# Two-layer graph attention on one core: the layout in DRAM of the split q and k, and the loads that read it

## The chip, the cores and the metric

One chip is a Trainium2 (trn2); the kernel runs on one of its cores. The metric is device time in microseconds (us) from the start to the end of the program, lower is better. A profile of one execution goes with it. In the profile PE is TensorE, PEld its weight load, DVE is VectorE, ACT is ScalarE, POOL is GpSimd and SP is SyncE; "L543" is line 543 of the kernel, and "SPq" or "ACTq" is an instruction of that engine's queue that issues a DMA.

## What is computed

16 graphs (batches) of 1024 nodes with 256 features each, all in float32, and an integer adjacency matrix for each. Layer 0 has 8 heads of 32 columns:

```python
q, k, v = heads(x @ Wq), heads(x @ Wk), heads(x @ Wv)       # (16, 8, 1024, 32)
e = einsum('whqd,whkd->whqk', q, k)
e = where(e >= 0, e, 0.2 * e)
attn = softmax(where(adj > 0, e, NEG), axis=-1)
h = layernorm(attn @ v, heads side by side)
x = x + layernorm(concat([h, x]) @ Wffn.T)
```

Layer 1 makes two graph attentions, in which the score of a pair of nodes is a sum of one number for each node, then a layer norm with the residual, a feed-forward of 1024 hidden units with ReLU, and a last layer norm with the residual.

## The kernel before

The kernel goes through the 16 batches in order. While the scores of batch b are worked on, the features, the mask and the projections of batch b + 1 are made ready, and what remains of batch b - 1 (output projection, the two graph attentions, feed-forward) is done in between. The order of all instructions on all engines is fixed when the kernel is built: each piece of work is a Python generator that says which engine it wants next and at what cost, and a planner (`Order`, with due times from `AIM`) picks the next one. Buffers are counted by pools of the same planner: a thread takes one and gives it back. At run time every engine, and every queue of an engine that issues DMAs, goes through its own list in order.

**Projections (`qk_part`, L446).** For each batch, each group g of 4 heads, o = 0 for q and 1 for k, and each half of the nodes, PE makes a tile of 128 rows (4 heads of 32 columns) by 512 nodes. ACT writes it rounded to `high` (L463), DVE writes the difference to `low` (L465). Both are buffers of the pool "pair" (18 buffers, 2 KB of each of the 128 partitions), which also holds the adjacency loads `adj_i` (L394, issued by ACT), the feature loads `xr` (L435, issued by ACT) and many intermediates. SyncE stores `high` and `low` to the DRAM tile `qk_halves` (L469), 256 KB each, and the thread gives the two buffers back.

**Stacks (`load_stacks`, L521).** For each head, SyncE makes four loads of 256 KB (L543) from `qk_halves` into the two tiles `qs` and `ks`, of 128 partitions by 1024 nodes each. `qs` holds q's 32 high rows and 32 low rows, twice; `ks` holds k's high rows twice in the upper 64 partitions and k's low rows twice in the lower 64. One matmul over 128 partitions thus gives (high + low of q) times (high + low of k). There are two pairs of stacks, so the loads of head h + 2 can start when the scores of head h are done. The planner prices the four issues at 500 ns each (L533, `load(4)`).

**Scores (`all_scores` L556, `weights` L583).** For each head and each of 8 tiles of 128 keys, two matmuls of 512 columns write 128 x 1024 scores (L576). ACT or DVE scales them by 0.2 (L594, L592; DVE only in batch 0), DVE takes the maximum with the scores (L596), ACT takes the exponential (L599), and GpSimd multiplies by the mask (L603), which needs that half of the mask from all 8 adjacency tiles. PE then multiplies by v (L623), and `after_head` transposes the sums (L649) and divides.

**Beginning.** Batch 0 has nothing before it that could cover its projections, its mask and its first stacks. In it `prepare` (L1008) also loads and folds the other weights ("setup", loads at L283 and L1026 to L1029 on SyncE, PE at L1044 to L1082).

The `general_path` at the end of the file is run only if a check of value ranges fails, and takes no part here.

Of the kernel before, what the change touches and what calls it, by code (L numbers as in the profile page):

```python
# [9 lines left out]
FT = mybir.dt.float32  # L10
# [10 lines left out]
P = 128  # L21
# [156 lines left out]
def on(shared=False, delay=0.0, **costs):  # L178
    return "on", (costs, shared, delay)
# [6 lines left out]
def wait(event):  # L186
    return "wait", event


def fire(event):  # L190
    return "fire", event


def take(pool):
    return "take", pool


def give(pool):
    return "give", pool


def start(thread, aim):
    return "start", (thread, aim)
# [21 lines left out]
def unshifted_path(  # L225
# [8 lines left out]
    nc = tc.nc  # L234
    B, N, D = x.shape
# [3 lines left out]
    DH = D // H  # L239
# [4 lines left out]
    G = 4  # L244
# [19 lines left out]
    dram = ctx.enter_context(tc.tile_pool(name="dram", bufs=3, space=bass.MemoryType.DRAM))  # L264
# [4 lines left out]
    def misc(dtype=FT):  # L269
        return psum.tile([P, HALF], dtype, tag="misc", name="ps_m", bufs=bufs["misc"])  # L270

    def buf(shape, tag, name, dtype=FT):
        return sb.tile(shape, dtype, tag=tag, name=name, bufs=bufs[tag])
# [44 lines left out]
    def load(n=1, latency=3500):  # L318

        return on(SP=500 * n, delay=latency)  # L320
# [59 lines left out]
    scratch = {}  # L380
# [65 lines left out]
    def qk_part(b, g, o, nh):  # L446

        w = (wq, wk)[o]
        cols = slice(nh * HALF, (nh + 1) * HALF)
        for u in range(nh * 2, nh * 2 + 2):  # L450
            yield wait(("xT", b, u))
        yield take("stage")
        yield take("pair")
        yield take("pair")
        yield take("misc")
        pa = misc()
        high, low = (buf([P, HALF], "pair", n) for n in ("high", "low"))
        yield on(PE=1720)
        for dc in range(DC):
            nc.tensor.matmul(pa, w[:, dc, g * P:(g + 1) * P], xTs[b][:, dc, cols],  # L460
                             start=(dc == 0), stop=(dc == DC - 1))
        yield on(ACT=590)
        nc.scalar.copy(high.bitcast(FR), pa)  # L463
        yield on(DVE=690)
        nc.vector.tensor_tensor(low, pa, high, op=OP.subtract)  # L465
        yield give("misc")
        yield load(2)
        for i, part in enumerate((high, low)):
            nc.sync.dma_start(scratch[b, g][o, i, :, cols], part)  # L469
        yield give("pair")  # L470
        yield give("pair")
        yield give("stage")
        yield fire(("qk", b, g, o, nh))

    def project_qk(b, g, t0):
        scratch[b, g] = dram.tile([2, 2, P, N], FT, name="qk_halves")
        for o in range(2):
            for nh in range(NH):
                yield start(qk_part(b, g, o, nh), t0 + (2 * o + nh) * AIM["qk_step"] * SLOT)
# [31 lines left out]
    def project(b, t0):  # L511
        yield take("xT")
        xTs[b] = buf([P, DC, N], "xT", "xT")
        for u in range(NP):
            yield start(x_pair(b, u), t0 + (AIM["x"] + AIM["x_step"] * u) * SLOT)
        yield start(make_mask(b, t0), t0 + 0.5 * SLOT)
        for g in range(H // G):
            yield start(project_qk(b, g, t0 + AIM[("qk0", "qk1")[g]] * SLOT), t0)
            yield start(project_v(b, g, t0 + AIM[("v0", "v1")[g]] * SLOT), t0 + (0.8, 1.0)[g] * SLOT)

    def load_stacks():  # L521


        for b in range(B):
            for h in range(H):
                yield take("stacks")
                both = [sb.tile([P, N], FR, tag=name, name=name, bufs=bufs["stacks"]) for name in ("qs", "ks")]
                stacks[b, h] = both
                for o in range(2):
                    for nh in range(NH):  # L530
                        yield wait(("qk", b, h // G, o, nh))
                d = scratch[b, h // G]
                yield load(4)  # L533
                for o in range(2):
                    for i in range(2):

                        rows = slice((h % G) * DH, (h % G + 1) * DH)
                        if o == 0:
                            src = d[0, :, rows, :]
                        else:  # L540
                            s = d[1, i, rows, :]
                            src = bass.AP(tensor=s.tensor, offset=s.offset, ap=[[0, 2], [N, DH], [1, N]])
                        nc.sync.dma_start(both[o][i * 2 * DH:(i + 1) * 2 * DH, :].bitcast(FT), src)  # L543
                yield fire(("stack", b, h))

# [543 lines left out]
    with tc.manual_schedule():  # L1089
        for dst, w in ((wq, Wq), (wk, Wk), (wv, Wv)):  # L1090
            load_w(dst, w)
        work.add(project(0, -SLOT), 0.0)
        work.add(load_stacks(), 0.0)
        work.add(all_scores(), 0.0)
        work.add(all_values(), 0.0)
        work.add(prepare(), 0.5 * SLOT)
        work.run()
# [308 lines left out]
```

## Time and profile before

| | before |
|---|---|
| time, median of 3 runs | 4614.92 us (4610.21 to 4616.06) |
| span of the profiled execution | 4611.1 us |
| PE busy | 4364.5 us, 95% |
| DVE, ACT, POOL busy | 3267.0, 2895.1, 2451.1 us |
| granted TensorE clock, mean | 0.982 |
| DMA | 343.54 MB, mean 75 GB/s |
| loads of stacks (L543) | 512 of 256 KB, issued by SyncE |
| stores of halves (L469) | 256 of 256 KB, issued by SyncE |

Busy time is a sum over the span; a mean over 4.6 ms does not tell whether all stretches look alike, so views of single stretches go with it. A wait in the profile is put down to the instruction whose end came last before the waiting instruction began. A granted clock below 1.00 means that the matmuls of that stretch ran slower.

### The profile page before, as it was taken

Reading aid. Unit: us, or ns where it says so; the run is one execution under the profiler, and the core shown is the slowest. Engines: PE = TensorE matmul, PEld = TensorE weight load, DVE = VectorE, ACT = ScalarE, POOL = GpSimd, SP = SyncE. Lnnn points to the kernel's source line nnn. Section 1 sums busy time; section 2 is a strip of 40 time slices with the busy share of each in tenths; the row PEclk is TensorE's granted clock in tenths of the full one; section 3 lists DMA queues with packets and bytes.
Section 4 is the critical chain, followed back from the end, with each engine's and each line's share of the span. In section 5 each row is a group of like instructions: output and inputs, shape, how many; then the busy total and the mean of one; then the engine's idle time right before and its main releaser. Section 6 shows DMA issues by size and latency. Waiting matters only on the chain.

```text
span 4611.1 us, 57125 instructions
## 1 busy us (share of the span) xinstructions
PE 4364.5 (95%) x20298; PEld 2930.7 (64%) x20298; DVE 3267.0 (71%) x5246; ACT 2895.1 (63%) x4030; POOL 2451.1 (53%) x1544
## 2 busy tenths in 40 slices
PE   5788899999999999999999999999999999999999
PEld 2344466766667666666766667676666766666587
DVE  2666777777678776777777677777767876777754
ACT  2556567666666666666666666666666666666631
POOL 1565556556555655555456555555655465565710
PEclk7889999999999999999999999999999999999999
DMA  4311212212121221212122121221213122121100
GB/s 136 113 52 64 95 59 82 79 57 99 63 102 57 79 84 61 102 61 95 60 78 84 68 102 61 87 73 66 93 64 106 59 77 83 60 98 44 40 21 20
DMA packets 151940, 343.54 MB, mean 75 GB/s; under 512 B 17504, under 2 KB 20064, under 8 KB 151648
## 3 DMA queue, kind: packets, MB, share of 16 engines
q1 hardware_dynamic: 105568, 255.90, 15.1%
q10 hardware_dynamic: 46080, 83.91, 5.9%
q8 instruction: 164, 2.69, 0.2%
q14 instruction: 128, 1.05, 0.1%
HBM read 239.09 MB, written 100.66 MB: 74 GB/s over the span
## 4 chain that ended last, share of the span: by engine, by line
PE 62%; DVE 17%; DMA 8%; issue 5%; POOL 5%; ACT 3%; SPq 0%; ACTq 0%; POOLq 0%; DVEq 0%
PE ps_a L623 13%; PE ps_s L576 8%; PE ps_m L847 8%; PE ps_m L912 7%; PE ps_m L940 7%; PE ps_m L872 5%; DVE att L810 4%; POOL p L603 4%; DVE att L813 4%; DVE p L596 4%; DMA ks<-qk_halves 3%; DMA adj_i<-in_adj_dram 3%; PE ps_m L757 3%; PE ps_m L725 2%; PE ps_m L728 2%
## 5 line engine op out<-in xcount | busy, mean ns | idle before, releaser
L603 POOL TENSOR_TENSOR p<-p,mask 128x1024 f32<-128x1024 f32 x1024 | 2209.6, 2174 | 1715.5 <-ACT p L599 1547.4
L596 DVE TENSOR_TENSOR p<-p,ps_s 128x1024 f32<-128x1024 f32 x1024 | 1210.2, 1213 | 417.8 <-ACT p L594 417.0
L599 ACT ACTIVATE p<-p 128x1024 f32<-128x1024 f32 x1024 | 1080.8, 1058 | 447.2 <-DVE p L596 412.3
L594 ACT ACTIVATE p<-ps_s 128x1024 f32<-128x1024 f32 x993 | 973.4, 1025 | 223.0 <-PE ps_s L576 179.3
L623 PE MATMUL ps_a<-p,v 128*64 128x512 f32 x4096 | 1020.2, 615 | 50.2 <-POOL p L603 48.2
L576 PE MATMUL ps_s<-qs,ks 128*128 128x512 f32 x2048 | 633.1, 429 | 62.1 <-DVE p L596 37.0
L623 PEld LDWEIGHTS ps_a<-p,v 128*64 128x64 f32 x4096 | 246.0, 137 | 540.7 <-issue 384.7
L576 PEld LDWEIGHTS ps_s<-qs,ks 128*128 128x128 f32 x2048 | 352.3, 191 | 357.9 <-DVE p L596 103.7
L872 PE MATMUL ps_m<-y,att 128*128 128x256 f32 x2048 | 483.3, 382 | 16.3 <-ACT v L497 13.6
L940 PE MATMUL ps_m<-wf,hid 128*128 128x256 f32 x2048 | 475.7, 382 | 9.0 <-ACT xT L309 8.7
L912 PE MATMUL ps_m<-rT,wf 128*128 128x256 f32 x2048 | 475.6, 381 | 0.4 <-DVE rT L368 0.4
L847 PE MATMUL ps_m<-y,att 128*128 128x258 f32 x2048 | 472.4, 381 | 1.5 <-DVE hn L656 1.5
L940 PEld LDWEIGHTS ps_m<-wf,hid 128*128 128x128 f32 x2048 | 380.7, 191 | 77.9 <-issue 15.3
L872 PEld LDWEIGHTS ps_m<-y,att 128*128 128x128 f32 x2048 | 377.4, 190 | 81.9 <-ACT v L497 16.3
L847 PEld LDWEIGHTS ps_m<-y,att 128*128 128x128 f32 x2048 | 386.0, 190 | 65.3 <-issue 4.6
L810 DVE SCALAR_TENSOR_TENSOR att<-first,second 128x1024 f32<-128x1024 f32 x256 | 353.1, 1379 | 82.0 <-ACT first L797 82.0
L912 PEld LDWEIGHTS ps_m<-rT,wf 128*128 128x128 f32 x2048 | 379.4, 191 | 49.5 <-PE ps_m L649 0.8
L813 DVE SCALAR_TENSOR_TENSOR att<-mask,att 128x1024 f32<-128x1024 fp8e4 x256 | 328.0, 1281 | 8.7
L818 ACT ACTIVATE y<-y,check 128x258 f32<-128x258 f32 x256 | 130.8, 511 | 290.1 <-DVE check L816 268.5
L400 DVE TENSOR_SCALAR adj_b<-adj_i 128x512 fp8e4<-128x512 int32 x256 | 226.9, 918 | 99.0 <-DMA adj_i<-in_adj_dram 99.0
L334 POOL TENSOR_SCALAR rs<-mv 128x2 f32<-128x2 f32 (+1 forms) x224 | 57.2, 255 | 416.0 <-DVE mv L331 415.9
L921 ACT ACTIVATE hid<-ps_m,bf 128x256 f32<-128x256 f32 x383 | 163.5, 472 | 132.6 <-PE ps_m L912 104.6
(100 smaller groups left out, 4256.9 us busy)
## 6 DMA issues: line engine op xcount, KB each, us to landing
adj_i<-in_adj_dram ACTq DMA_DIRECT2D x256, 256.0 KB
qs<-qk_halves SPq DMA_DIRECT2D x256, 256.0 KB
ks<-qk_halves SPq DMA_DIRECT2D x256, 256.0 KB
qk_halves<-high SPq DMA_DIRECT2D x128, 256.0 KB
qk_halves<-low SPq DMA_DIRECT2D x128, 256.0 KB
xr<-in_x_dram ACTq DMA_DIRECT2D x64, 256.0 KB
x_kept<-x SPq DMA_DIRECT2D x64, 256.0 KB
x<-x_kept SPq DMA_DIRECT2D x64, 256.0 KB
```

Source lines behind the costliest of these rows:

```text
L576: nc.tensor.matmul(ps[i][:, cols], kk[:, t * P:(t + 1) * P], q[:, cols], start=True, stop=True)
L594: nc.scalar.activation(p, ps, AF.Copy, scale=ALPHA)
L596: nc.vector.tensor_tensor(p, p, ps, op=OP.max)
L599: nc.scalar.activation(p, p, AF.Exp)
L603: nc.gpsimd.tensor_tensor(p, p, mask_of(b, t), op=OP.mult)
L623: nc.tensor.matmul(acc[nh * 64:(nh + 1) * 64, :], v[:, t, c:c + 64], p[:, nh * HALF:(nh + 1) * HALF], start=(t == 0), stop=(t == NT - 1))
L810: nc.vector.scalar_tensor_tensor(e, first[:, 0, :], second[:, j:j + 1], first[:, 1, :], op0=OP.mult, op1=OP.max)
L813: nc.vector.scalar_tensor_tensor(e, mask_of(b, j), -1.0, e, op0=OP.mult, op1=OP.mult, accum_out=sums[:, j:j + 1])
L847: nc.tensor.matmul(pa[:, cols:cols + width], big[:, j, i * P:(i + 1) * P], rows[:, j, :width], start=(j == 0), stop=(j == NT - 1))
L872: nc.tensor.matmul(pa[:, i * D:(i + 1) * D], big[:, j, t * P:(t + 1) * P], y2[:, j, :D], start=(j == 0), stop=False)
L912: nc.tensor.matmul(pa[:, i * 2 * P:(i + 1) * 2 * P], wf1[:, dc, hc * P:(hc + 1) * P], rT[:, dc, :], start=(dc == 0), stop=(dc == DC - 1))
L940: nc.tensor.matmul(pa[:, i * D:(i + 1) * D], hid[hc // 2][:, hc % 2, i * P:(i + 1) * P], wf2[:, hc, :], start=(hc == 0), stop=False)
```

## The change

The dimensions of the DRAM tile `qk_halves` are put in another order: before, [q or k][high or low][128 rows][1024 nodes], and after, [q or k][128 rows][high or low][1024 nodes]. The stores follow it. A load for `qs` reads 64 rows of one piece of DRAM, in which high and low alternate; before it read two blocks of 32 rows. A load for `ks` reads 32 rows, each of them twice in succession; before it read a block of 32 rows, twice. The purpose is that the access patterns of these loads have 64 or 32 rows as outermost dimension and no longer 2. In the stacks the rows stand in another order, the same one in `qs` and in `ks`.

```diff
-            nc.sync.dma_start(scratch[b, g][o, i, :, cols], part)
+            nc.sync.dma_start(scratch[b, g][o, :, i, cols], part)
...
-        scratch[b, g] = dram.tile([2, 2, P, N], FT, name="qk_halves")
+        scratch[b, g] = dram.tile([2, P, 2, N], FT, name="qk_halves")
...
-                        rows = slice((h % G) * DH, (h % G + 1) * DH)
+                        rows = d[o, (h % G) * DH:(h % G + 1) * DH]
                         if o == 0:
-                            src = d[0, :, rows, :]
+                            src = rows.rearrange("d i n -> (d i) n")
                         else:
-                            s = d[1, i, rows, :]
-                            src = bass.AP(tensor=s.tensor, offset=s.offset, ap=[[0, 2], [N, DH], [1, N]])
+                            src = bass.AP(tensor=rows.tensor, offset=rows[:, i, :].offset,
+                                          ap=[[2 * N, DH], [0, 2], [1, N]])
                         nc.sync.dma_start(both[o][i * 2 * DH:(i + 1) * 2 * DH, :].bitcast(FT), src)
```

## The prediction

> **What bounds the kernel now.** I read the page first (TensorE busy 95% of the span, DMA far from full), then busy time by stage, because an average over 4.6 ms hides a start that differs from the rest. Columns of a row: stretch, length, then busy time and instruction count of PE, PEld, DVE, ACT and POOL, granted clock, DMA share, GB/s.
>
> ```profile
> 36.00:64.50 28.50, 4.46 (x15) 1.80 (x15) 2.05 (x4) 2.19 (x5) 0.00 (x0) 0.61 0.41 135
> 64.50:120.00 55.50, 30.96 (x90) 12.18 (x91) 23.38 (x25) 19.11 (x25) 19.11 (x9) 0.72 0.31 101
> ...
> 174.00:205.00 31.00, 17.21 (x71) 6.44 (x70) 16.74 (x20) 16.04 (x20) 19.20 (x10) 0.89 0.36 117
> ...
> 727.00:1000.00 273.00, 267.87 (x1265) 181.24 (x1264) 202.06 (x325) 182.30 (x254) 152.31 (x96) 1.00 0.22 78
> ```
>
> There are two regimes. From about 690 us on, every batch takes 273 us and PE is busy for 267.9 of it at clock 1.00: PE-bound. The list of PE's waits between 1000 and 4003 us (eleven batches) has no DMA in it; it opens with
>
> ```profile
> PE ps_m L409 <- DVE low L465: 17.5, 11, 1.6
> PE ps_m L872 <- ACT v L497: 10.7, 11, 1.0
> ```
>
> that is, one wait of each kind per batch. Before 600 us PE often idles, at a lower clock. So the question is what the loads cost in the first 600 us. Their rate can be read where they run almost alone, in the DMA view of 294 to 334 us (40 slices of 1 us; the loads of one head are issued from 294.92 to 299.4):
>
> ```profile
> DMA  1001111111111111111111110000000000005000
> GB/s 45 0 8 41 37 37 45 49 49 53 53 49 57 49 49 57 49 49 57 49 49 57 49 45 8 0 16 0 0 0 8 0 0 0 0 0 233 29 0 0
> ```
>
> The four loads (4 x 256 KB = 1.05 MB) take until 318 us at 49 to 57 GB/s and a busy share of one tenth: two engines of sixteen. The single 256 KB transfer at 330 us runs at 233 GB/s. The timeline of SyncE shows the second effect: issues stall while the two engines are full, and what comes next in SyncE's order stalls too (a pair of issues costs 1.0 us when nothing blocks).
>
> ```profile
> 37.49 5.79 SPq L543 DMA_DIRECT2D ks<-qk_halves  x2
> ...
> 162.93 6.32 SPq L543 DMA_DIRECT2D ks<-qk_halves  x2
> 169.30 6.72 SPq L283 DMA_DIRECT2D setup<-in_L_gnn_Wffn_dram  x1
> ```
>
> Third, the timelines of PE and ACT show who waits (in brackets: idle time before, and releaser).
>
> ```profile
> 64.49 2.05 PE L576 MATMUL ps_s<-qs,ks 128*128 128x512 f32 x4 [18.25 <-DMA ks<-qk_halves]
> ...
> 192.74 0.69 PE L1044 MATMUL ps_m<-ident,setup 128*128 128x128 f32 x2 [8.63 <-DMA setup<-in_L_gnn_Wffn_dram]
> ...
> 223.68 2.05 PE L576 MATMUL ps_s<-qs,ks 128*128 128x512 f32 x4 [5.82 <-DMA ks<-qk_halves]
> ...
> 579.18 1.12 PE L649 MATMUL ps_m<-ident,ho 128*128 128x128 f32 x4 [8.65 <-ACT v L497]
> ```
>
> ```profile
> 81.52 1.06 ACT L599 ACTIVATE p<-p 128x1024 f32<-128x1024 f32 x1 [6.64 <-DMA qs<-qk_halves]
> ...
> 116.66 1.02 ACT L594 ACTIVATE p<-ps_s 128x1024 f32<-128x1024 f32 x1 [13.38 <-issue]
> ...
> 578.74 0.39 ACT L497 ACTIVATE v<-ps_m 128x256 f32<-128x256 f32 x1 [4.73 <-DMA ks<-qk_halves]
> ```
>
> ACT does not read the stacks. It waits because it issues the adj_i loads (L394) in its own order: such a load needs a "pair" buffer, buffers of that pool also hold "high" and "low" until their store has landed, and the stores share rings with the stack loads. The chain of waits says it for the 13.4 us:
>
> ```profile
> 92.12 23.53 DMA ks<-qk_halves
> 115.64 0.02 issue
> 115.67 0.02 ACTq L394
> ```
>
> **What the Trainium skill says.** "DMA: Bandwidth & Descriptors", section "Why a DMA increments its semaphore by 16 and not by 1": the number of engines is the largest k up to 16 that divides the slowest dimension (size 1 left out) of both access patterns; its "Rules for kernel authors" name a leading broadcast of c copies as confining a transfer to c engines. That gives 2 for both old patterns (outermost 2 against 64 partitions) and agrees with the tenth of busy share above. It gives 16 for the new ones (64 against 64, and 32 against 64); no trace of before shows that. Section "Queues, rings and completion order" of the same page: on each engine descriptors are consumed in ring order, so a store issued behind stack loads waits for its share on those two engines; the two chain lines agree.
>
> **The change, part by part.**
>
> *Loads, 512 of 256 KB.* Bytes, count and issuing engine stay; the engines go from 2 to 16. Cost of a head's four loads now: 24 us. After: from above, 16 times an engine's 53/2 = 26.5 GB/s, 424 GB/s, gives 2.5 us; from below, the stretch 2 to 8 us moves 284 GB/s at share 0.95 with 2 KB rows, 299 GB/s in full, 3.5 us. With issues (4 x 0.5 us) and landing I take 6 us, 5 to 8.
>
> *Stores, 256.* Rows of 2 KB as before, 128 partitions outermost, so their engines stay; only the row pitch in DRAM grows from 4 to 8 KB. I price this at nothing: they land beside compute, which waits on them only through freed buffers. At worst the rate halves, some 1 us more for each.
>
> *Order of rows in the stacks.* q's high and low now alternate with d, and so does k's repeat; the same sum over 128 rows, the same matmuls. The order of instructions does not move, since the planner's price for the loads (L533) is not edited. No wait is added.
>
> *(a) First score, 64.49 us.* Its loads are issued from 36.1 us. After, issues end at 38.1. Ahead are four stores (1.05 MB, issued from 33.2) and two adj_i loads (0.5 MB): with the stacks 2.6 MB, at 300 GB/s about 9 us from 34 us, so landed about 44. Gain 20.
>
> *(b) Head 0, 64.5 to 119 us.* The ACT stall of 6.6 goes (the stores are out by 43, landed before ACT wants buffers). The last mask chunk of batch 0 (adj_i issued at 95.03, used by DVE at 101.99) lands in 5 us in place of 7: 2. The 13.4 us ACT stall hides mostly under four GpSimd products (103.4 to 111.7); the scores at 118.99 would otherwise have gone at 116: 3. Together 11.
>
> *(c) 120 to 307 us.* PE's wait for the setup load, 8.6, goes: that load was issued at 169.3 behind a blocked SyncE and landed behind a head's loads. The ks wait, 5.8, goes. Two mask transposes waiting for adj_b (1.3 and 2.0): 3.2 together. Sum 18. The rest stays: near its end this stretch is spaced by GpSimd (L603, 2174 ns each, POOL busy 139.9 us from 64.5 to 306.6).
>
> *(d) Batch 1, 307 to 690 us.* The 8.65 at 579 goes, as ACT there is held up by the ks loads (6.04 and 4.73 just before). Waits for xr (4.3 at 366, 3.5 at 644) shrink by 3 in all, since the first runs beside a head's loads. Sum 12.
>
> *(e) Clock.* The four matmuls after the 18 us gap take 2.05 us, later ones 1.20. Fewer gaps mean fewer slow restarts: 4 us, an estimate from some five such places.
>
> *(f) Steady batches and tail.* DVE waits for adj_i 99 us in all, which must shrink, but DVE has 71 us free of each 273, and no PE wait there ends in a DMA. Zero.
>
> Sum: 20 + 11 + 18 + 12 + 4 = 65, so 4614.9 - 65 = **4550 us**.
>
> **The rivals.** *Small gain, 4582.* Only waits that PE itself has on these transfers return (18.3 + 5.8 + 8.6 = 33); what ACT and SyncE lost is taken over by GpSimd. For it: several (b) and (c) gaps already end in POOL waits. Against: the last chain lines and the 8.65 at 579 put the hold-up of ACT on these loads.
>
> *Large gain, 4520.* With loads prompt, batch 0 is paced by its engines alone. DVE and POOL each have 140 us of work in 64.5 to 306.6; at 78% of the busier one that is 180 us, not 242: 62, with (a) and (d) 94. For it: the heads' period of 26 to 31 us lies close to the 24 us of a load. Against: from 235 to 307 heads still take 24 us, and PE waits for no load there.
>
> *Slower, 4625 or more.* Stores at the larger pitch, or short full-width bursts in the way of adj_i, hold up the steady batches: it would take 5 us in each of 15 to eat the gain and add 10. For it: a batch has 5.2 us of PE idle time, so no slack on PE. Against: DMA share there is 0.22, and transfers at full width leave the rings sooner. The skill's row on HBM pitch ("Latency and other measured facts") starts its losses from 512 KiB; here it is 8 KB, and no run here shows the loss.
>
> *No change* would need the loads to stay at two engines, for instance if contiguous rows were merged again.
>
> **How the numbers follow.** Forecast 0.60, large gain 0.20, small gain 0.15, no change 0.02, slower 0.03. Faster 0.95, same 0.02, slower 0.03. Range 4500 to 4588: down to a large gain with one more 20 us of the 140 us that PE idles from 36 to 580, up past the small one.
>
> **What would show it.** Right: a head's loads at over 250 GB/s for 3 to 4 us in place of two dozen slices of about 50; issues of ks at 0.5 us each; first score near 44 us; PE's waits for ks and for setup gone; end of batch 0 (306.6 now) near 255; 273 us in each steady batch. Wrong: loads still at 53 GB/s; first score after 55; a steady batch other than 273; or the gaps of (b) and (c) kept, with POOL or DVE as releaser.

## The result, and the profile after

| | before | after |
|---|---|---|
| time, median of 6 runs each | 4611.02 us | 4532.44 us |
| ratio to before, 95% interval | | 0.9826 [0.9813, 0.9839] |
| span of the profiled execution | 4611.1 us | 4531.4 us |
| first scores on PE | 64.49 us | 45.95 us |
| head 0 of batch 0 done (L649) | 120.01 us | 88.98 us |
| head 7 of batch 0 done (L649) | 306.63 us | 264.80 us |
| one product of batch 1's first graph attention (L847) | 692.18 us | 638.25 us |
| the same product twelve batches on | 3968.62 us | 3890.36 us |

The gain is 78.6 us where 65 was forecast. The last five rows of the table are landmarks, single instructions whose start is compared in the two profiles. They divide the gain: 18.5 us at the first scores, 31.0 at the end of head 0, 41.8 at the end of batch 0, 53.9 in batch 1. From there on it keeps growing, to 78.3 at 3890 us: (3968.62 - 692.18) / 12 = 273.04 us for a batch became (3890.36 - 638.25) / 12 = 271.01.

The DMA view of 252 to 292 us of the changed kernel (40 slices of 1 us; one head's loads are issued at 253.1 to 255.5):

```profile
DMA  0069998000000000000000000000000000004200
GB/s 0 0 123 295 238 217 176 0 0 0 0 0 0 0 0 0 0 0 0 0 0 0 0 0 0 0 16 0 0 0 8 0 0 0 0 0 168 94 0 0
```

The same 1.05 MB that took 24 slices at about 50 GB/s are through in five, with 0.6 to 0.9 of the sixteen engines' time taken while they run. The rate is 210 GB/s in the mean of the five. How many engines took part can be counted. The packet lines of the two pages, before and then after (each count of small packets contains the one before it):

```profile
DMA packets 151940, 343.54 MB, mean 75 GB/s; under 512 B 17504, under 2 KB 20064, under 8 KB 151648
```

```profile
DMA packets 159108, 343.57 MB, mean 76 GB/s; under 512 B 24672, under 2 KB 27232, under 8 KB 158816
```

There are 7168 more packets, all under 512 B, and 7168 is 512 loads times 14: one small packet more, in each load, for each of 14 engines that joined the two. The Trainium skill has the reason ("DMA: Bandwidth & Descriptors", section "Why a DMA increments its semaphore by 16 and not by 1"): each engine that takes part posts its own increment of the completion semaphore. In every run below this count tells, to within 5 packets, how many loads ran on sixteen engines ("wide" in the code cuts) and how many on two ("narrow").

In SyncE's timeline the two ks loads of a head, which took 5.8 and 6.3 us to issue before, take 2.58 us for the first head and 1.24 for the second:

```profile
36.87 2.58 SPq L543 DMA_DIRECT2D ks<-qk_halves  x2
...
51.46 1.24 SPq L543 DMA_DIRECT2D ks<-qk_halves  x2
```

In PE's timeline the 18.25 us in front of the first scores is 1.58 us; the 8.65 us gap in batch 1, put down to ACT, is gone.

```profile
45.95 2.04 PE L576 MATMUL ps_s<-qs,ks 128*128 128x512 f32 x4 [1.58 <-DMA ks<-qk_halves]
```

A steady batch, 271 us (stretch, length, busy time and count of PE, PEld, DVE, ACT and POOL, clock, DMA share, GB/s):

```profile
638.00:909.00 271.00, 267.46 (x1264) 181.00 (x1263) 203.87 (x325) 182.21 (x253) 152.39 (x97) 1.00 0.27 78
```

PE's work is nearly the same as in the batch of 273 us (267.9 us busy): over the twelve batches its busy time is 0.4 us less for each, with the same 15169 instructions. The other 1.6 of the 2.0 us were idle time, and the list of PE's waits from 947 to 3927 us (eleven batches; us in total, times, longest) says which: it now opens with

```profile
PE ps_m L872 <- ACT v L497: 10.7, 11, 1.0
PE ps_m L940 <- ACT xT L309: 8.0, 11, 0.7
```

The line that stood above these before, the mask transpose L409 waiting for DVE's `low` (L465), 17.5 us in eleven batches or 1.6 in each, is no longer there.

### The profile page after: what moved, and what is told of

Read it like the earlier page. It is cut to its first block, busy times and chain, and to the rows that moved or that the text cites. A ratio compares the mean times of both kernels' runs of the same rounds, so it can differ in the third digit from the quotient of the medians.

```text
span 4531.4 us, 57125 instructions
## 1 busy us (share of the span) xinstructions
PE 4348.7 (96%) x20298; PEld 2924.8 (65%) x20298; DVE 3304.5 (73%) x5246; ACT 2893.6 (64%) x4030; POOL 2454.6 (54%) x1544
## 2 busy tenths in 40 slices
DMA packets 159108, 343.57 MB, mean 76 GB/s; under 512 B 24672, under 2 KB 27232, under 8 KB 158816
## 3 DMA queue, kind: packets, MB, share of 16 engines
q14 instruction: 128, 1.05, 0.1%
## 4 chain that ended last, share of the span: by engine, by line
PE 72%; DVE 15%; POOL 5%; issue 4%; ACT 2%; DMA 0%; ACTq 0%; POOLq 0%; SPq 0%; DVEq 0%
PE ps_a L623 16%; PE ps_s L576 10%; PE ps_m L872 8%; PE ps_m L847 8%; PE ps_m L912 7%; PE ps_m L940 7%; DVE att L810 5%; POOL p L603 5%; DVE att L813 5%; PE ps_m L460 3%; DVE p L596 3%; PE ps_m L757 3%; PE ps_m L725 2%; PE ps_m L728 2%; PE ps_m L351 2%
## 5 line engine op out<-in xcount | busy, mean ns | idle before, releaser
L847 PE MATMUL ps_m<-y,att 128*128 128x258 f32 x2048 | 472.3, 381 | 2.9 <-DVE hn L656 2.9
L847 PEld LDWEIGHTS ps_m<-y,att 128*128 128x128 f32 x2048 | 385.9, 190 | 66.7 <-issue 6.0
L400 DVE TENSOR_SCALAR adj_b<-adj_i 128x512 fp8e4<-128x512 int32 x256 | 249.7, 1020 | 15.5 <-DMA adj_i<-in_adj_dram 15.5
```

Source lines behind the costliest of these rows:

```text
L847: nc.tensor.matmul(pa[:, cols:cols + width], big[:, j, i * P:(i + 1) * P], rows[:, j, :width], start=(j == 0), stop=(j == NT - 1))
```

## The experiments

Each was timed against the kernel before on the same chip. The medians of the kernel before lay between 4611.0 and 4614.8 us on the chips of these runs, so times of runs from different chips compare to some 4 us.

**Outermost 2, with blocks that adjoin.** The first attempt to give the new layout two engines again wrote the 64 rows as two blocks of 32 (for k, two blocks of 16), in all batches or in some only. Shortened to the lines that hold where `ways` is 2:

```diff
-                            src = rows.rearrange("d i n -> (d i) n")
+                            src = bass.AP(tensor=rows.tensor, offset=rows.offset,
+                                          ap=[[2 * DH // ways * N, ways], [N, 2 * DH // ways], [1, N]])
...
-                                          ap=[[2 * N, DH], [0, 2], [1, N]])
+                                          ap=[[2 * N * DH // ways, ways], [2 * N, DH // ways], [0, 2], [1, N]])
```

All batches (`ways` = 2):

> New layout and new row order kept; only the access patterns of the loads are written with an outermost dimension of 2 (two blocks of 32 or 16 rows). Theory A (the number of engines is the cause): back to before, 4611 us within 8; a head's four loads run about 24 us at 50 GB/s, first score near 64 us, 273.0 us for each steady batch. Theory B (the layout or the locality of rows in DRAM is the cause): near after, 4532 us.

Batches 2 to 15 only:

> New layout; 64 or 32 rows outermost for batches 0 and 1 only, outermost 2 in batches 2 to 15. Theory A with two separate parts (start 54 us, steady batches 2.0 us each): 4532 + 26 = 4558 us, steady batches 273.0 us. Rival C (the gain of the start is lost again later, since PE-bound batches take what they take): above 4590 us.

Batches 0 and 1 only:

> New layout; outermost 2 in batches 0 and 1, 64 or 32 rows outermost in batches 2 to 15. Theory A with two separate parts: 4611 - 26 = 4585 us, first score near 64 us, steady batches 271.0 us. Rival D (the shorter steady batches are a consequence of the other start, not of the loads in them): steady batches 273.0 us and 4611 us.

Measured, in this order: 4534.2, 4531.6 and 4533.1 us, ratios 0.9826, 0.9821 and 0.9824. That reads like theory B, but the packet counts forbid it: all three have 159108 packets, exactly as the changed kernel, so the loads ran on sixteen engines. The two blocks adjoin in memory, so they can be described as one dimension of 64 rows (32 for k); at which step they were joined is not shown. These runs test neither theory; they repeat the change three times, at 4532 to 4534 us.

**The old layout on sixteen engines.** Layout, stores and order of rows as before; eight loads of 32 rows in place of four.

```diff
-                        if o == 0:
-                            src = d[0, :, rows, :]
-                        else:
-                            s = d[1, i, rows, :]
-                            src = bass.AP(tensor=s.tensor, offset=s.offset, ap=[[0, 2], [N, DH], [1, N]])
-                        nc.sync.dma_start(both[o][i * 2 * DH:(i + 1) * 2 * DH, :].bitcast(FT), src)
+                        for j in range(2):
+                            to = (2 * i + j) * DH
+                            nc.sync.dma_start(both[o][to:to + DH, :].bitcast(FT), d[o, i if o else j, rows, :])
```

> Old layout and old row order kept; each load is split into two of 32 rows (128 KB), so eight for a head, each with 32 rows outermost. Theory A: near after, 4532 to 4542 us, the difference being four more issues for each head on SyncE (about 0.3 us each); 271 us for each steady batch. Theory B: near before, 4611 us.

Measured: 4531.1 us, ratio 0.9817 [0.98, 0.9833], with 167305 packets, which fits 1024 loads on sixteen engines. This is the whole gain without the new layout. The four extra issues for each head cost nothing that shows.

**The new layout on two engines.** The loads read the new layout in the old order of rows, so the two outer blocks lie apart and can't become one.

```diff
-                            src = rows.rearrange("d i n -> (d i) n")
+                            src = rows.rearrange("d i n -> (d i) n") if wide else rows.rearrange("d i n -> i d n")
...
-                                          ap=[[2 * N, DH], [0, 2], [1, N]])
+                                          ap=[[2 * N, DH], [0, 2], [1, N]] if wide else [[0, 2], [2 * N, DH], [1, N]])
```

With `wide = False`:

> New layout in DRAM with its stores, but the loads in the old order of rows (high block, then low block; k's block twice), so 2 is the outermost dimension of their patterns and the two blocks don't adjoin. Theory A (the number of engines): 4611 us within 8, a head's loads near 24 us, first score near 64 us, steady batches 273.0 us. Theory B (layout and pitch of rows): 4532 us.

Measured: 4615.0 us, ratio 1.0002 [0.9993, 1.001], 151940 packets, first scores at 63.47 us. Together the two runs answer the question. The number of engines carries the effect: the old layout on sixteen has all of the gain, the new one on two has none. Layout, pitch of the stores and order of rows carry nothing that shows beyond 0.1%.

**Where in the run.** `wide = b < 2`, then `wide = b >= 2`:

> As n1_two_engines for batches 2 to 15, as the changed kernel for batches 0 and 1. Theory A with two separate parts (start 54 us, steady batches 2.0 us each): 4532 + 26 = 4558 us, steady batches 273.0 us. Rival C (the gain of the start is lost later): above 4590 us.

> As n1_two_engines for batches 0 and 1, as the changed kernel for batches 2 to 15. Theory A with two separate parts: 4611 - 26 = 4585 us, first score near 64 us, steady batches 271.0 us. Rival D (shorter steady batches follow from the other start): steady batches 273.0 us, 4611 us.

Measured: 4570.5 us, ratio 0.9912 [0.9895, 0.9928], and 4574.1 us, ratio 0.9913 [0.9897, 0.993]. The first is 12.5 us over what was expected, the second 10.9 under it. The losses against 4532 us still add up, 38 and 42, against 79 for both. Steady batches are as theory A has them, 273.04 and 271.02 us, so C and D fall. The misses lie in where the line was drawn. Heads 0 and 1 of batch 2 are loaded in the middle of batch 1's work (at 527 to 557 us before, at 484 to 513 in the first kernel), but count as batch 2. At the product in batch 1 the first kernel is 43.2 us ahead of before (649.00 against 692.18) and the second 11.9 (680.26); together 55.1, against the 53.9 of the change. The first kernel's PE timeline keeps the gap in batch 1 that the change removes:

```profile
535.58 1.11 PE L650 MATMUL ps_m<-ident,ho 128*128 128x128 f32 x4 [8.07 <-ACT v L497]
```

It stood at 579.18 with 8.65 us before; line numbers are one higher in this kernel.

**One head, in the steady batches.** In the trace of before, head 7's loads (issued from 1331 us in one batch) are still under way when ACT issues two adj_i loads at 1348.1 and 1348.6. The DMA view of 1330 to 1370 us (slices of 1 us) has the 45 to 57 GB/s of two engines from 1337 to 1342 and again at 1347 and 1348; in the slices between, other transfers run beside them:

```profile
DMA  4354064111111367311688217451127941272111
GB/s 172 107 166 100 12 178 145 51 53 47 57 49 49 82 244 184 133 45 53 201 256 322 96 51 281 139 199 43 49 104 256 344 184 61 74 213 80 55 49 51
```

DVE's timeline there:

```profile
1352.00 0.60 DVE L400 TENSOR_SCALAR adj_b<-adj_i 128x512 fp8e4<-128x512 int32 x1
1354.48 1.38 DVE L400 TENSOR_SCALAR adj_b<-adj_i 128x512 fp8e4<-128x512 int32 x1 [1.88 <-DMA adj_i<-in_adj_dram]
1355.78 1.21 DVE L596 TENSOR_TENSOR p<-p,ps_s 128x1024 f32<-128x1024 f32 x1
1356.91 0.68 DVE L465 TENSOR_TENSOR low<-ps_m,high 128x512 f32<-128x512 f32 x1
```

DVE waits 1.88 us for a transfer, and `low`, two instructions later, comes behind that wait; PE's next transpose waits for `low` at 1357.64. So PE's wait has a DMA at its root, one step behind the releaser that its own line names. The test takes the changed kernel and makes only head 7 of batches 1 to 15 slow (`wide = not (b > 0 and h == 7)`):

> The changed kernel, with the loads of head 7 alone (batches 1 to 15) in the old pattern on two engines. In the trace of before only this head's loads run while the two adj_i loads are under way that DVE then waits for ahead of the low of L465 and the mask transpose of L409. Theory E (the steady gain is this one wait): all of it is lost, 2.0 us in each steady batch, 273.0 us each, 4532 + 26 = 4558 us, and PE's wait L409 <- DVE low is back at 1.6 us for each batch. Rival F (the gain is spread over the eight heads): an eighth is lost, 4535 us, steady batches 271.3 us.

Measured: 4556.8 us, ratio 0.9875 [0.9859, 0.9892]; (3912.29 - 637.86) / 12 = 272.87 us for a batch. Its DVE and PE timelines have both waits again:

```profile
1299.90 1.08 DVE L400 TENSOR_SCALAR adj_b<-adj_i 128x512 fp8e4<-128x512 int32 x1 [2.18 <-DMA adj_i<-in_adj_dram]
```

```profile
1302.76 0.38 PE L409 MATMUL ps_m<-ident_b,adj_b 128*128 128x128 bf16 x4 [1.59 <-DVE low L465]
```

The reverse, only head 7 wide (`wide = h == 7`):

> The reverse of n7_head_7_narrow: the loads of head 7 alone run on sixteen engines, in all batches, those of the other seven heads on two. Theory E (the steady gain is this one wait): 271.0 us for each steady batch with seven of eight heads slow, no wait L409 <- DVE low, first score near 64 us; 4613 - 26 = 4587 us. Rival F (the gain is spread over the eight heads): 272.7 us for each steady batch, 4610 us.

Measured: 4588.1 us, ratio 0.9942 [0.9925, 0.9958]; first scores at 63.28 us, (3945.89 - 693.74) / 12 = 271.01 us for a batch, and no such wait. One head in eight carries the whole steady gain; F falls. What the two runs leave open is the last link. SyncE issues two x loads (L694) right behind head 7's, in 5.94 us before, 5.93 with head 7 narrow and 1.06 with head 7 wide. Whether adj_i was held up by the head's loads themselves or by these x loads, which the head's loads delay, is not told apart.

**The first head alone.** `wide = not (b == 0 and h == 0)`:

> The changed kernel, with the loads of batch 0, head 0 alone on two engines. Theory A (the later first score is carried to the end): first score near 64 us, 4532 + 18 = 4550 us. Rival C (a later start is caught up, as batch 0 has idle time on every engine): 4532 to 4538 us.

Measured: 4552.6 us, ratio 0.987 [0.9853, 0.9886], 20 us above the change; first scores at 64.56 us, 18.6 late. Of this 2.7 us are caught up in head 0, and the rest is carried to the end: head 0 ends 15.9 us late, head 7 of batch 0 15.9, the product in batch 1 15.8, and the profiled execution 16.9. C falls here too.

**Half of the bytes.** q's loads wide (four of 32 rows), k's two loads on two engines.

```diff
                         if o == 0:
-                            src = rows.rearrange("d i n -> (d i) n")
-                        else:
-                            src = bass.AP(tensor=rows.tensor, offset=rows[:, i, :].offset,
-                                          ap=[[2 * N, DH], [0, 2], [1, N]])
+                            for j in range(2):
+                                to = (2 * i + j) * DH
+                                nc.sync.dma_start(both[o][to:to + DH, :].bitcast(FT), rows[:, j, :])
+                            continue
+                        src = bass.AP(tensor=rows.tensor, offset=rows[:, i, :].offset,
+                                      ap=[[0, 2], [2 * N, DH], [1, N]])
```

> New layout; q's loads on sixteen engines (four of 32 rows for a head), k's two loads on two engines, so half of the bytes take the narrow way. Theory A (time lost follows how long the two engines are full, now about 11 us for a head): head 7's loads are out of the two engines before the adj_i loads 17 us later, so 271.0 us for each steady batch; of the 54 us of the start 15 to 35 are lost: 4547 to 4567 us. Rival G (any narrow transfer in the way costs the same, however short): 4600 us or more and 273.0 us for each steady batch.

Measured: 4543.2 us, ratio 0.9849 [0.9833, 0.9866]; first scores at 58.58 us, (3897.91 - 646.88) / 12 = 270.92 us for a batch. The DMA view of 252 to 300 us (slices of 1.2 us) has the narrow part:

```profile
DMA  1100000004911111111110000000000000000050
GB/s 51 55 17 0 0 0 0 0 0 147 266 38 48 31 34 38 44 55 55 48 55 17 0 0 0 0 0 0 0 0 14 0 7 0 0 0 0 0 219 0
```

Eleven slices, 13 us, for half of a head. The steady gain is whole, and G falls; that the short loads are out of adj_i's way in time fits this, though the bytes on two engines and their time were not varied apart. The loss of the start is smaller than the lower end of 15: the first scores are 12.6 us late, head 7 of batch 0 9.3 and the product in batch 1 8.6.

## Why the prediction was right, and where it was not

By its own steps. A landmark moves for two reasons, less idle time of PE and less busy time for the same number of instructions, so the last column has the second:

| step | forecast, us | measured, us | read from | of this, PE busy time |
|---|---|---|---|---|
| (a) first scores | 20 | 18.5 | 64.49 to 45.95 | 0.6 |
| (b) head 0 | 11 | 12.5 | first scores to L649: 55.5 to 43.0 | 2.1 |
| (c) rest of batch 0 | 18 | 10.8 | L649 to L649: 186.6 to 175.8 | 1.9 |
| (d) batch 1 | 12 | 12.1 | L649 to the product: 385.6 to 373.5 | 3.9 |
| (e) clock | 4 | in the others | | 8.5, the sum of these |
| (f) steady batches and tail | 0 | 24.7 | 78.6 less 53.9 | 4.5 in twelve batches |

- **Cause and mechanism of the start: right**, shown by the old layout on sixteen engines (0.9817) and the new one on two (1.0002). A head's loads were taken at 5 to 8 us; five slices, and a landing of ks 5.1 us after its issue in the median, agree. The two estimates of the transfer alone, 2.5 and 3.5 us, were too short: 1.05 MB at 210 GB/s is 5 us.
- **(a)** agrees within 2 us.
- **(b)** agrees in size; its parts add to 11.6, not 11. Not every part came as said. ACT's stall of 6.6 us is gone, but after the change ACT waits 4.98 us at 53.18, when its three xr issues take 5.89 us (1.31 before). The 13.4 us stall has no counterpart after (4.3 us there, put down to POOL). That it came from stores queued behind the stack loads is read from a chain that names a load of ks and no store. SyncE issued the stores of this time only at 102.5 to 110.6, behind an issue of 9.7 us at 92.6; their late issue would do as well, and it was not tried apart.
- **(c) was mis-sized**, 10.8 for 18. The waits for setup (8.6) and ks (5.8) went as said, 14.4 together. But the two transposes waiting for adj_b, priced at 3.2, still wait 1.25 and 1.98 us (1.26 and 1.98 before): DVE's own order holds them, no DMA. And new short waits took the place of others, so that all of PE's waits in the stretch shrank only by 8.8, from 46.6 to 37.8 us. Two of the new ones, in PE's timeline after:

```profile
99.18 0.43 PE L409 MATMUL ps_m<-ident_b,adj_b 128*128 128x128 bf16 x4 [2.91 <-DVE low L465]
...
185.77 0.59 PE L409 MATMUL ps_m<-ident_b,adj_b 128*128 128x128 bf16 x4 [1.98 <-DVE setup L307]
```

- **(d)** agrees within 0.1 us, and that is luck. The 8.65 us went as said. All 9.7 us that PE waited for xr went, where 3 were forecast; new waits for ACT (4.7 and 4.0 us) and longer ones for DVE took about as much back, and 3.9 us are busy time.
- **(e)** is in (a) to (d). If all of the 8.5 us of busy time is the clock, it was twice the forecast; the granted clock rose from 0.72 to 0.74 in (b), stayed at 0.87 in (c) and rose from 0.93 to 0.95 in (d). The one place that the prediction named did not change: the first four matmuls still take 2.04 us, after a wait of 1.6 us in place of 18.
- **(f) failed.** "Zero" rested on "DVE has 71 us free of each 273, and no PE wait there ends in a DMA". The free time is a sum; the wait sits at one place in DVE's fixed order. And the PE wait did have a DMA behind it, hidden by one step: its line, L409 waiting for `low`, stood in the prediction's own fence as the first entry. Narrowing head 7 alone brought it back (272.87 us a batch); widening head 7 alone removed it (271.01).
- **The signs.** Of those of being right, five slices took the place of two dozen, PE's waits for setup and for ks are gone but for 1.6 us ahead of the first scores, issues of ks take some 0.6 us each in most heads (1.3 in the first), and the first scores came at 45.95 for 44. But only one slice is over 250 GB/s, where 3 to 4 us were said; batch 0 ends at 264.8, not near 255; and "a steady batch other than 273", a sign of being wrong, came true with 271.0.
- **The rivals.** The small gain (33 us) fell: the start alone brought 53.9. The large gain (94 us, so 4520) lies nearer to the measured 4532 than the forecast does, but fell in its reason: it gave 62 us to (b) and (c), which brought 23.3, and heads of batch 0 still take 21.5 to 28 us. The slower case had the right place, steady batches without slack on PE, and the wrong sign.

That 4550 lies within 18 us of 4532 is in part luck. Steps (a) to (e) were 11 too high together, mostly by (c), and made up for some of the 25 of (f); another 3.9 us is the kernel before, at 4614.9 in three runs and 4611.0 in six.

## What to carry to other kernels

In this kernel, loads whose outermost dimension was 2 ran on two engines of sixteen. To find such loads, look for stretches in which the busy share sits at a tenth and the rate at a constant 50 GB/s. Then give the pattern an outermost dimension of many rows, by layout or by splitting the load: both brought the same time here. When you price what such loads delay, take a wait's named releaser as the last step only. Follow it back along its engine's own order until something is reached that was not itself waiting, above all on an engine that has no slack. An engine's free time over a whole batch says nothing about one instruction in a fixed order.

## What the runs showed of the hardware that was not expected

- **Sixteen engines were not eight times two.** Two engines moved 53 GB/s, 26.5 each. Spread over sixteen, the same head's loads ran at 176 to 295 GB/s in the four full slices, at a busy share of 0.8 to 0.9, so an estimated 12 to 20 GB/s for an engine while it was busy. Packet time on SyncE's queue rose from 15.1% to 20.0% of the sixteen engines' span for the same bytes. Why was not isolated. The median landing of k's loads, where each row is read twice, takes 5.1 us against 4.1 for q's, but they are also issued behind q's.
- **An outermost 2 in the code was not always one for the engines.** Two blocks that adjoin in memory ran as one dimension does (159108 packets with the pattern written as two blocks, 151940 with blocks that lie apart).
